# Gamma and beta of layer 0's normalization: two fused VectorE operations in place of two GpSimd operations

## The chip, the cores and the metric

One core of a Trainium2 chip runs the whole program. The metric is device time in microseconds, the median of several executions. The engines of a core have queues of their own that run in order and wait for each other by semaphores: TensorE (PE in the profile; its weight loads are PEld), VectorE (DVE), ScalarE (ACT), GpSimd (POOL) and SyncE (SP), whose queue issues most of the DMAs.

## The reference, cut to what matters

Two cross-attention layers follow each other on 4 x 1024 tokens of width 1024, all in f32. The change concerns the end of layer 0:

```python
# layer 0, after its attention
out = out @ Wo + bo
x = out + hidden_state
mu = jnp.mean(x, axis=-1, keepdims=True)
var = jnp.var(x, axis=-1, keepdims=True)
return (x - mu) * jax.lax.rsqrt(var + EPS) * gamma + beta
# layer 1, with a = norm(audio_kv) * ln_gamma + ln_beta
Q = hidden_states @ Wq.T;  K = a @ Wk.T;  V = a @ Wv.T
out = softmax(Q K^T / 8, masked) V @ Wo.T
return hidden_states + tanh(gate) * out
```

What layer 0 returns is read twice in layer 1: as the left operand of its scores and as the residual.

## The kernel before, in words

The 4096 tokens are 32 subtiles of 128 rows (NSUB); two subtiles are a pair (NPAIR = 16). The program has three parts. First, up to some 720 us, the queries of layer 0 and its attention run, mixed with the folding of layer 1's query weights. Then comes the stage of the change, layer 0's output projection, 16 pairs, with the folding of layer 1's output weights put between (L870, pairs 0 to 7). Last is layer 1, whose scores and outputs alternate by pairs.

A projection of one pair is `project` (L414). The 256 x 1024 by 1024 x 1024 product is made by a Strassen-like scheme: seven products of 128-row, 512-column halves, each four matmuls, into PSUM banks X, V and W that several outputs share. After a product VectorE adds the bank's present content to the rows of one output half (`add`, L430), and the next product accumulates into the same bank. So TensorE's next product into X must wait until VectorE has read X. The order on X is A11*B11, S2*T2, S1*T1, S4*B22; V takes S3*T3 and A22*N4, W takes A12*B21. The left operands S1, S2, S4 and A21-S3 are made by VectorE from the pair's `o` tile in `left_out` (L408 to L411), one pair ahead. In pair 10 and after, VectorE also forms sums of layer 1's weight blocks (L181 to L184, 128x2048 each).

The rows `r` of a pair are loaded from x by SP's queue (L894), and GpSimd adds the output bias bo to them (L895) ahead of the products. When a pair's seven products are added, its normalization runs as filler work between the products of the next pair: `close_rows` (L974) makes a list of steps for each of the two subtiles, and `project` pops a share of them after each product (`others`). The steps are: two bn_stats (L280), then the aggregate, the addition of eps and ScalarE's square root (L285 to L287), then reciprocal and (r - mean) * rstd (L290, L291), then `last`: GpSimd's multiplication by gamma (L977) and addition of beta (L978), and the store of the rows to x1 in DRAM by SP's queue (L979). gamma0_sb and beta0_sb are 128 x 1024 tiles, each row the same.

The r tiles of pairs 1 to 15 come from a pool of six buffers, so the load of a subtile of pair p waits until the x1 store of the same subtile of pair p - 3 has read its buffer. SP's queue issues in the order in which the planner put it; a DMA that waits holds what is behind it. The tile framework that builds the program settles the order of the instructions of each engine from its own estimate of times; bn_stats alone is marked to stay in program order.

Of the kernel before, what the change touches and what calls it, by code (L numbers as in the profile page):

```python
# [11 lines left out]
ALU = mybir.AluOpType  # L12
# [33 lines left out]
EPS0 = 1e-6  # L46
# [25 lines left out]
def tile_two_cross_attentions(  # L72
# [25 lines left out]
    nc = tc.nc  # L98

    def sub_ap(t):  # L100
        return slice(t * P, (t + 1) * P)
# [110 lines left out]
    for i in range(2):  # L212
        t = scratch.tile([P, H], F32, tag="cnat", name=f"ctx_{i}", bufs=2)
# [3 lines left out]
    for w, n in ((wk0, "wk0"), (wv0, "wv0")):  # L217
        t = wpool.tile([P, KC, 256], F32, tag="wb", name=n)
# [3 lines left out]
    def constant(ap, shape, name, dt=F32, pool=const):  # L222
        t = pool.tile(shape, dt, tag=name, name=name)
        nc.sync.dma_start(out=t, in_=ap)
        return t
# [45 lines left out]
    nc.vector.tensor_copy(key_bias, mask1_sb)  # L271
    nc.vector.tensor_scalar(key_bias, key_bias, 1.0, -MASKED, ALU.subtract, ALU.mult)

    def normalize_steps(t, eps, name, late=False):
        st = small.tile([P, 2, 6], F32, tag="st", name=f"st_{name}")
        mv = small.tile([P, 2], F32, tag="mv", name=f"mv_{name}")
        rstd = small.tile([P, 1], F32, tag="rstd", name=f"rstd_{name}")

        def stats(i):
            r = nc.vector.bn_stats(st[:, i, :], t[:, i * 512 : (i + 1) * 512])  # L280
            if late:
                tc.keep_in_program_order(r)

        def deviation():
            nc.vector.bn_aggr(mv, st.rearrange("p a b -> p (a b)"))  # L285
            nc.vector.tensor_scalar(rstd, mv[:, 1:2], eps, None, ALU.add)
            nc.scalar.activation(rstd, rstd, AF.Sqrt)  # L287

        def scale():
            nc.vector.reciprocal(rstd, rstd)  # L290
            nc.vector.tensor_scalar(t, t, mv[:, 0:1], rstd, ALU.subtract, ALU.mult)  # L291

        return [lambda: stats(0), lambda: stats(1), deviation, scale]

    def transpose_ctx(layer):

# [35 lines left out]
    for i in range(2):  # L332
        run(normalize_steps(cnat[i], EPS1, f"ctx{i}", True))
# [475 lines left out]
    steps = query_steps(0, rows)  # L809
# [135 lines left out]
    last = NSUB - SUB  # L945
# [8 lines left out]
    for c in range(2):  # L954
# [12 lines left out]
    gamma0_sb, beta0_sb = (  # L967
        constant(ap.partition_broadcast(P), [P, H], n, F32, c2)
        for ap, n in ((gamma0, "gamma0"), (beta0, "beta0"))
    )  # L970
# [2 lines left out]

    def close_rows(pair, r):  # L974
        def last(u):
            t = pair * 2 + u
            nc.gpsimd.tensor_tensor(r[u], r[u], gamma0_sb, ALU.mult)  # L977
            nc.gpsimd.tensor_tensor(r[u], r[u], beta0_sb, ALU.add)  # L978
            nc.sync.dma_start(out=x1[pair][sub_ap(u), :], in_=r[u])  # L979

        steps = []
        for u in range(2):
            steps += normalize_steps(r[u], EPS0, f"0_{pair * 2 + u}", True) + [lambda u=u: last(u)]
        return steps

    lefts = {}
# [22 lines left out]
    for pair in range(NPAIR):  # L1009
        r, a = ahead_r, ahead_a  # L1010
# [26 lines left out]

        project(a, w_o, r, fill, tail=tail)
        fill = close_rows(pair, r)
        if pair == NPAIR - 2:  # L1040
            xq = load_x1(0)
# [80 lines left out]
    for pair in range(NPAIR):  # L1122
        r = []
# [84 lines left out]
```

## Time and profile before

| what | us |
|---|---|
| median of 3 runs | 1946.02 (1945.31 to 1955.23) |
| the profiled execution, its own time | 1946.74 |
| its span, first to last instruction | 1944.5 |
| TensorE busy, share of the span | 1885.5 (97%) |
| VectorE busy | 1276.9 (66%) |
| ScalarE busy | 384.7 (20%) |
| GpSimd busy | 288.4 (15%) |
| L291, least, median and most of 32 | 0.804, 0.812, 2.956 |
| L977, least, median and most of 32 | 2.342, 2.347, 2.808 |
| L978, least, median and most of 32 | 2.342, 2.357, 4.276 |

The page lists groups of instructions by line, engine and operation, with busy time, mean duration, and the idle time of the engine before them with what ended it. The timeline lists instructions by start; a bracket at the end of a row is the idle time before it and what ended it. The chain that ended last follows the end of the program backwards from each instruction to what released it. The table of stretches gives busy time by engine, TensorE's granted clock as a share of full speed, and the DMA's busy share and rate. One matmul of the source appears as two records in the timeline.

### The profile page before, as it was taken

To read this page: it belongs to the slowest core of one execution; us is meant where nothing else is said; L and a number is where in the kernel's file an instruction comes from. 1 tells how busy PE (TensorE), PEld (TensorE's weight loads), DVE (VectorE), ACT (ScalarE), POOL (GpSimd) and SP (SyncE) were. 2 spreads that over 40 slices of the span, in tenths; PEclk is the share of its full clock that TensorE was granted. 3 is DMA by queue.
4 is the path that set the end of the run, shared out by engine and by line. 5 is a ranking of instruction groups with operands and counts; after the bars stand their busy time and mean duration, and the time that the engine had idled before them with its cause. 6 is when DMAs were issued, how large, how long until landed. Compare 5 with 4: busy or idle time off the path is not lost.

```text
span 1944.5 us, 17115 instructions
## 1 busy us (share of the span) xinstructions
PE 1885.5 (97%) x6160; PEld 892.9 (46%) x6160; DVE 1276.9 (66%) x1540; ACT 384.7 (20%) x1028; POOL 288.4 (15%) x198
## 2 busy tenths in 40 slices
PE   8999999998998889999999999999999999999999
PEld 7744444444445654433443444444444444444444
DVE  3424798898877974454467667557665766576653
ACT  1111554553435761121100001000000000000000
POOL 0000111111100004345445642000000000000000
PEclk9999999999998889999999999999999999999999
DMA  8971689798778885666672335374747474747421
GB/s 278 181 191 65 175 246 262 229 255 243 227 184 247 251 259 187 206 214 201 198 217 98 129 98 140 108 178 124 184 119 184 119 183 125 178 127 176 119 87 43
DMA packets 218180, 342.10 MB, mean 176 GB/s; under 512 B 25456, under 2 KB 140528, under 8 KB 213104
## 3 DMA queue, kind: packets, MB, share of 16 engines
q1 hardware_dynamic: 156736, 255.03, 46.6%
q10 hardware_dynamic: 52544, 46.14, 8.6%
q0 software_dynamic: 8816, 39.85, 7.0%
q8 instruction: 48, 0.79, 0.2%
q14 instruction: 36, 0.29, 0.1%
HBM read 203.34 MB, written 137.63 MB: 175 GB/s over the span
## 4 chain that ended last, share of the span: by engine, by line
PE 81%; DVE 11%; DMA 3%; issue 2%; ACT 2%; SPq 0%; POOL 0%; DVEq 0%; ACTq 0%
PE wx L422 59%; PE wx L558 12%; PE big L662 2%; DVE mx L673 2%; DVE s L666 2%; PE wx L361 1%; PE big L361 1%; PE big L870 1%; DVE s L676 1%; DVE sm L693 1%; DMA q<-qTd 1%; DVE pT L398 1%; DMA pq<-p 1%; DVE s L697 1%; PE wx L843 1%
## 5 line engine op out<-in xcount | busy, mean ns | idle before, releaser
L430 DVE TENSOR_TENSOR r<-wx,r 128x512 f32<-128x512 f32 x224 | 153.8, 687 | 265.5 <-PE wx L422 259.8
L484 ACT ACTIVATE s<-s 128x1024 f32<-128x1024 f32 x32 | 33.7, 1057 | 651.8 <-DVE s L483 642.9
L434 DVE TENSOR_TENSOR s<-wx,key_bias 128x512 f32<-128x512 f32 x64 | 44.2, 690 | 137.2 <-PE wx L422 137.2
L558 PE MATMUL wx<-xT,wq_S 128*128 128x512 f32 x256 | 119.3, 601 | 0.8 <-ACT z L569 0.8
L895 POOL TENSOR_TENSOR r<-r,bo 128x1024 f32<-128x1024 f32 x32 | 78.4, 2458 | 275.1 <-DMA r<-in_x_dram 168.3
L422 PE MATMUL wx<-wo_B,S 128*128 128x512 f32 x256 | 116.7, 599 | 0.9 <-DVE r L430 0.9
L558 PE MATMUL wx<-xB,wq_A 128*128 128x512 f32 x256 | 116.4, 599 | 0.0
L422 PE MATMUL wx<-b_B,pT 128*128 128x512 f32 x256 | 115.8, 593 | 0.6 <-ACT pT L393 0.6
L422 PE MATMUL wx<-b_B,S_p 128*128 128x512 f32 x256 | 116.0, 596 | 0.0
L422 PE MATMUL wx<-a_B,xT 128*128 128x512 f32 x256 | 115.4, 592 | 0.0
L422 PE MATMUL wx<-a_B,S_x 128*128 128x512 f32 x256 | 115.3, 593 | 0.0
L422 PE MATMUL wx<-wo_B,o 128*128 128x512 f32 x256 | 113.5, 595 | 0.0
L680 ACT ACTIVATE s<-s,mx 128x64 f32<-128x64 f32 x304 | 101.1, 335 | 55.2 <-DVE mx L673 49.0
L666 DVE TENSOR_TENSOR s<-big,m 128x1024 f32<-128x1024 f32 x64 | 77.0, 1218 | 41.1 <-PE big L662 41.1
L977 POOL TENSOR_TENSOR r<-r,gamma 128x1024 f32<-128x1024 f32 x32 | 76.5, 2389 | 134.5 <-DVE r L291 134.5
L662 PE MATMUL big<-kv,q 64*128 64x128 f32 x1024 | 86.4, 301 | 10.2 <-DMA q<-qTd 10.0
L662 PEld LDWEIGHTS big<-kv,q 64*128 64x128 f32 x1024 | 75.0, 205 | 44.8 <-issue 36.8
L978 POOL TENSOR_TENSOR r<-r,beta 128x1024 f32<-128x1024 f32 x32 | 80.5, 2514 | 2.4
L398 DVE STREAM_TRANSPOSE pT<-pq 128x1024 f32<-128x1024 f32 x66 | 77.9, 1219 | 1.7 <-DMA pq<-p 1.7
L422 PEld LDWEIGHTS wx<-wo_B,S 128*128 128x128 f32 x256 | 47.3, 190 | 66.6 <-issue 52.9
L697 DVE TENSOR_TENSOR s<-s,sm 128x1024 f32<-128x1024 f32 x64 | 76.8, 1220 | 0.9
L422 PEld LDWEIGHTS wx<-wo_B,o 128*128 128x128 f32 x256 | 48.0, 190 | 63.5 <-issue 63.1
(159 smaller groups left out, 2984.9 us busy)
## 6 DMA issues: line engine op xcount, KB each, us to landing
p<-s POOLq DMA_DIRECT2D x19, 1024.0 KB, 8.6
pq<-p POOLq DMA_DIRECT2D x76, 256.0 KB, 6.0
xq<-in_x_dram SPq DMA_DIRECT2D x64, 256.0 KB, 10.0
q<-qTd SPq DMA_DIRECT2D x32, 512.0 KB, 6.5
oTd<-oT ACTq DMA_DIRECT2D x32, 512.0 KB, 6.7
ad<-a SPq DMA_DIRECT2D x16, 1024.0 KB, 5.8
o<-oTd SPq DMA_DIRECT2D x16, 1024.0 KB, 8.7
r<-in_x_dram SPq DMA_DIRECT2D x32, 512.0 KB, 4.3
```

What stands on the lines that cost most here:

```text
L398: nc.vector.transpose(dst.rearrange("p k (u i) -> p k u i", i=Q), t[:, :, k0 * Q : k1 * Q].rearrange("p u (k j) -> p k u j", j=Q),)
L422: nc.tensor.matmul(bank, a[s][:, k, :], w[m][:, k, :], start=first and k == 0, stop=last and k == HK - 1, skip_group_check=True,)
L430: nc.vector.tensor_tensor(at, bank, at, ALU.add)
L434: nc.vector.tensor_tensor(at, bank.rearrange("p (h s) -> p h s", s=S), bias.unsqueeze(1).to_broadcast([P, 512 // S, S]), ALU.add,)
L558: nc.tensor.matmul(bank, w_q[a][:, k, sub_ap(i)], rows[b][:, k, :], start=first and k == 0, stop=last and k == HK - 1, skip_group_check=True,)
L662: nc.tensor.matmul(ps[:, at : at + P], q[on, c * 4 + g, :], k0bd[on, b, c, :], start=True, stop=True,)
L666: nc.vector.tensor_tensor(quarters[:, :, c * 8 : (c + 1) * 8], ps.rearrange("p (k a l) -> p a k l", a=NQ, l=Q), mask.rearrange("p e (h l) ...
L680: nc.scalar.activation(heads[:, 0, k], heads[:, 0, k], AF.Exp, bias=mx[:, 0, k : k + 1], accum_out=sm[:, 0, k : k + 1],)
L697: nc.vector.tensor_tensor(heads[:, e], heads[:, e], wide(sm[:, e]), ALU.mult)
L895: nc.gpsimd.tensor_tensor(ru, ru, bo_sb, ALU.add)
L977: nc.gpsimd.tensor_tensor(r[u], r[u], gamma0_sb, ALU.mult)
L978: nc.gpsimd.tensor_tensor(r[u], r[u], beta0_sb, ALU.add)
```

## The change: what it does

The multiplication by gamma and the addition of beta leave GpSimd. VectorE computes the same value in two operations with two tensors and one scalar per row: r = (r - mean) * gamma in place of r = (r - mean) * rstd, and then r = r * rstd + beta as a step of its own. The normalization of the context rows keeps the old form. `last` is only the store.

```diff
-    def normalize_steps(t, eps, name, late=False):
+    def normalize_steps(t, eps, name, late=False, scaled=None):
 ...
         def scale():
             nc.vector.reciprocal(rstd, rstd)
-            nc.vector.tensor_scalar(t, t, mv[:, 0:1], rstd, ALU.subtract, ALU.mult)
-
-        return [lambda: stats(0), lambda: stats(1), deviation, scale]
+            if not scaled:
+                nc.vector.tensor_scalar(t, t, mv[:, 0:1], rstd, ALU.subtract, ALU.mult)
+                return
+            nc.vector.scalar_tensor_tensor(t, t, mv[:, 0:1], scaled[0], ALU.subtract, ALU.mult)
+
+        def shift():
+            nc.vector.scalar_tensor_tensor(t, t, rstd, scaled[1], ALU.mult, ALU.add)
+
+        return [lambda: stats(0), lambda: stats(1), deviation, scale] + ([shift] if scaled else [])
 ...
     def close_rows(pair, r):
         def last(u):
-            t = pair * 2 + u
-            nc.gpsimd.tensor_tensor(r[u], r[u], gamma0_sb, ALU.mult)
-            nc.gpsimd.tensor_tensor(r[u], r[u], beta0_sb, ALU.add)
             nc.sync.dma_start(out=x1[pair][sub_ap(u), :], in_=r[u])
 
         steps = []
         for u in range(2):
-            steps += normalize_steps(r[u], EPS0, f"0_{pair * 2 + u}", True) + [lambda u=u: last(u)]
+            steps += normalize_steps(
+                r[u], EPS0, f"0_{pair * 2 + u}", True, (gamma0_sb, beta0_sb)
+            ) + [lambda u=u: last(u)]
         return steps
```

In the changed kernel the two fused operations are lines 295 and 298, and the lines behind them in the file have numbers that are 7 higher in the functions between (L430 is L437 there, L408 to L411 are L415 to L418).

## The prediction

> **What bounds the kernel now.** I read the page first: who is busy, and which rows the change touches. Columns of the rows: busy us, mean ns of one, then the idle time before it.
>
> ```profile
> PE 1885.5 (97%) x6160; PEld 892.9 (46%) x6160; DVE 1276.9 (66%) x1540; ACT 384.7 (20%) x1028; POOL 288.4 (15%) x198
> L895 POOL TENSOR_TENSOR r<-r,bo 128x1024 f32<-128x1024 f32 x32 | 78.4, 2458 | 275.1 <-DMA r<-in_x_dram 168.3
> L977 POOL TENSOR_TENSOR r<-r,gamma 128x1024 f32<-128x1024 f32 x32 | 76.5, 2389 | 134.5 <-DVE r L291 134.5
> L978 POOL TENSOR_TENSOR r<-r,beta 128x1024 f32<-128x1024 f32 x32 | 80.5, 2514 | 2.4
> L697 DVE TENSOR_TENSOR s<-s,sm 128x1024 f32<-128x1024 f32 x64 | 76.8, 1220 | 0.9
> ```
>
> TensorE is the bound, 97% of the span. The change removes the rows L977 and L978, 157 us of GpSimd; L895 stays. None of that is TensorE time, so the question is what TensorE loses in the stage where these rows stand (layer 0's projection, 722 to 1165 us). The table of busy time by stretch, cut at the starts of the pairs, tells it (length, PE, PEld, DVE, ACT, POOL, clock, DMA share, GB/s):
>
> ```profile
> 960.70:1009.70 49.00, 49.00 (x114) 20.98 (x113) 31.91 (x47) 0.81 (x4) 26.50 (x11) 1.00 0.85 236
> 1009.70:1038.70 29.00, 24.65 (x58) 10.26 (x56) 23.86 (x26) 0.41 (x2) 16.50 (x6) 0.98 0.45 173
> 1038.70:1065.90 27.20, 27.20 (x57) 11.74 (x58) 16.18 (x24) 0.41 (x2) 16.69 (x7) 0.89 0.16 58
> 1065.90:1090.30 24.40, 24.40 (x57) 10.42 (x56) 12.04 (x23) 0.41 (x2) 11.49 (x5) 1.00 0.30 108
> ```
>
> A pair without value matmuls takes 24.47 us, two of them 49.0. One takes 29.0, with 4.35 us of idle TensorE, and the next 27.2 at a clock of 0.89. A fourth, from 1090.3, takes 25.4. Pairs 1 to 7, which carry value matmuls (L870), take 29.4 each and wait only for ScalarE. So VectorE costs the stage 4.5 + 2.7 + 0.95 = 8.2 us. The timelines of TensorE, then VectorE, then GpSimd say how:
>
> ```profile
> 1038.69 2.07 PE L422 MATMUL wx<-wo_T,o 128*128 128x512 f32 x2 [4.35 <-DVE o L410]
> 1102.76 2.41 PE L422 MATMUL wx<-wo_B,S 128*128 128x512 f32 x5 [0.87 <-DVE r L430]
> ```
> ```profile
> 1028.12 4.40 DVE L184 TENSOR_TENSOR a_N<-a_B,a_T 128x2048 f32<-128x2048 f32 x1
> ...
> 1033.04 2.24 DVE L408 TENSOR_TENSOR S<-o 128x512 f32<-128x512 f32 x1
> 1035.32 2.71 DVE L409 TENSOR_TENSOR S<-S,o 128x512 f32<-128x512 f32 x1
> 1037.95 0.68 DVE L410 TENSOR_TENSOR o<-o 128x512 f32<-128x512 f32 x1
> ```
> ```profile
> 750.73 9.29 POOL L895 TENSOR_TENSOR r<-r,bo 128x1024 f32<-128x1024 f32 x4 [8.14 <-DMA r<-in_x_dram]
> ...
> 1028.03 2.34 POOL L978 TENSOR_TENSOR r<-r,beta 128x1024 f32<-128x1024 f32 x1
> 1030.33 7.15 POOL L895 TENSOR_TENSOR r<-r,bo 128x1024 f32<-128x1024 f32 x2
> ```
>
> VectorE was stretched: L184 took 4.40 where its kind takes 2.29, L408 and L409 took 2.24 and 2.71 where 0.69 is normal, while GpSimd ran beta and two bo adds beside them. The three stretches add 5.7 us; TensorE waited 4.35 for the L410 behind them. The groups by form show whom GpSimd holds up, the same operation beside it (S) and in layer 1, where GpSimd is idle (S_x):
>
> ```profile
> L411 DVE TENSOR_TENSOR S<-o,S 128x512 f32<-128x512 f32 x16 | 29.0, 1810 | 0.0
> L411 DVE TENSOR_TENSOR S_x<-xT,S_x 128x512 f32<-128x512 f32 x16 | 11.0, 685 | 0.0
> ```
>
> L430, which has one operand in PSUM, stays at 687, and bn_stats (L280) at 681. Stretched are operations with two SBUF tensors, and L291.
>
> **The change, part by part.**
> *Removed on GpSimd:* 64 instructions, 157 us, none on the path. With them go the stretches above, and the wait of the x1 stores (L979, SP queue) for beta. The store of r and the next load of that buffer behind it come earlier, and so does the bo add, which no longer queues behind gamma and beta. Worth up to 8.2 us.
>
> *Added on VectorE:* for each of 32 subtiles one tensor_scalar of 0.81 us becomes two fused operations (L295 and L298 of the changed kernel). The trace has none of that kind. Bounds: 0.81 us below (L291's form; unlikely with a second tensor to read); 2.28 us above. The upper end is a rule against this change: the Trainium skill, "Vector Engine (DVE) Microarchitecture Reference", section 7, says that a scalar-tensor-tensor operation with two non-bf16 sources in SBUF runs at half throughput. Twice 1024 elements at the 0.96 GHz of "VectorE: DVE Perf Modes" plus L697's 0.15 us of fixed cost is 2.28 (an estimate). The nearest row, L697 with two SBUF f32 operands of 1024, shows 1.22, which is one element per cycle. I take 1.22: that row shows both operands arriving at full rate. VectorE gains 32 x (2.44 - 0.81) = 52 us of work; at 16 to 19 of 24.5 us per pair it is still not full.
>
> *Where the new work lies.* In the built order a pair's first half on VectorE is: add to X (L430), two bn_stats, aggregate, L286, L295, reciprocal, L298, then the next add to X, for which TensorE's S1*T1 product waits. Counted from a pair's first S3*T3 matmul (1065.85), the undisturbed pair of before shows where that add must be done:
>
> ```profile
> 1068.89 0.81 DVE L291 TENSOR_SCALAR r<-r,mv,rstd 128x1024 f32<-128x1024 f32 x1
> 1070.64 0.69 DVE L430 TENSOR_TENSOR r<-wx,r 128x512 f32<-128x512 f32 x1 [0.94 <-PE wx L422]
> ```
>
> L286 ends at 2.55; L295 2.6 to 3.8 (it needs no rstd, so ScalarE's root lies under it), reciprocal to 4.0, L298 to 5.2, add to 5.9. S1*T1 starts at 7.1 (1072.96). Slack 1.2 us, so alone the two cost nothing. (gamma and beta are issued at 722.1 and 733.3 and landed by 738, before the first L295 near 757.) Before, the add ended at 5.5. The second half has more: the add before the S4 product now has nothing ahead of it (before, one bn_stats), and the second subtile's L298 ends at 18.4, before the last add at 21.2. In pair 10 the planner puts the two 2.3 us weight sums ahead of that add, but also all of A22*N4 ahead of S4 on TensorE: the add ends near 13 without disturbance, S4 starts at 14.1.
>
> *The bo adds that remain* (32 x 2.35 us) can hold up the fused operations, which have two SBUF tensors. "SBUF — State Buffer", "Who interferes with whom", calls it an exclusive lock for a whole instruction; the trace agrees (2.83 us for the L291 at 757.74). One collision delays by up to 2.35 us; beyond the slack it stalls TensorE by 0.7 to 1.25 us. When does a bo add come? A store lands in 2.9 us, a load in 4.1 (median issue to landing in this stage), so 7.1 us after its L298. For the first subtile that is 12.4: it delays left_out (L408 to L411) and the second L298 to 20.6, harmless. For the second it is 27.7. In a pair of 29.4 us that lies between pairs: free. In one of 24.47 it is 3.3 of the next: GpSimd takes its turn after L295, L298 waits to 6.15 and ends at 7.35, the add at 8.0, a stall of 0.95. One by one: pair 1 (the four bo adds from 750.73 run to about 760) 1.25; pairs 4 and 6 (their load stands behind four bd stores in SP's queue, bo add at about 2.1) 0.7 each; pair 10 (two bo adds push the weight sums) 1.1; pair 11 0.25; pairs 12, 13, 14 0.95 each. Pair 9's load shares the DMA with a_B, 2, 3, 8 and 15 have none at that time. Sum 6.9 us. At the end of the stage four fused operations precede the add that the second score product waits for: 1171.7 against 1171.65, 0.1 us.
>
> *The clock.* "TensorE: Matmul & The Clock Gate", Part 1, halves the clock after an idle window of about 3.4 us. The row agrees for the 4.35 us gap (0.89 in the pair after it); after the gap of 0.87 the 5 us stretches show 1.00. Had each short stall the long one's surcharge (2.7/4.35), 6.9 would be 11; I take 6.9.
>
> *Sum.* The profiled execution took 1946.74 us (span 1944.5 and 2.2 around it), 0.7 over the median of 1946.02. 1946.7 - 8.2 + 6.9 + 0.1 = 1945.5; against the median, 1945.
>
> **The rivals.**
> *The bo adds miss the fused operations* (loads a microsecond later or earlier than I place them; L298 never caught). For: only 71 us of bo adds is left in 443, and a bo add coming before 1.5 or after 5.2 is free. Against: the period is regular, so one hit repeats. 1946 - 8 = 1938 to 1940.
>
> *The late VectorE chain of pair 10 and 11 stays.* For: four weight sums of 2.3 us stand there, and L417 for pair 11 ends at about 24 of 24.5 us; one bo add there makes TensorE idle again, and over 3.4 us the clock falls. Then 4 to 7 of the 8.2 are not saved: 1949 to 1954.
>
> *Slower: the fused operation runs at half rate.* Place: first half of each pair. At 2.28 us L298 ends at 7.35 and S1*T1 waits 0.95 in 14 pairs, 13 us. The slack being gone, the hits count in full, some seven of 2.1, 15 us; the add at the end of the stage comes 4.3 late, with clock 7 us. 1946 - 8 + 35 = 1973. It decides from about 1.8 us per operation, where the slack of 1.2 is used up. For: the sentence quoted. Against: L697.
>
> *A hidden transfer:* x1 is stored earlier, but the chain that ended last has no x1 load in this stage, so nothing is gained: inside the forecast.
>
> **How the numbers follow.** Forecast 0.58; bo adds miss 0.17; late chain 0.12; half rate 0.13. Within 0.5% (9.7 us; about what a measurement can tell from no change) is 1936.3 to 1955.7. Faster needs more than the 8.2 that VectorE costs the stage: 0.03. Slower is half rate and a tail of the late chain: 0.16. Same 0.81. The range runs from the misses, 1937, to the late chain, 1957; half rate is left out. The forecast's own range is 1941 to 1950.
>
> **What would show it.** Right: L295 and L298 at a least time of 1.22, means above 1.3; L411 (L418 there) nearer 0.7 than 1.81; no gap of over 2 us near 1038, clock 1.00; short waits of the S1*T1 weights on VectorE's add in pairs 12 to 14; GpSimd at about 131 us. Wrong: L298 at 2.3, a gap behind L417, or pairs at 24.47 throughout.

## The result, and the profile after

The changed kernel took 1940.2 us, the median of 20 runs (1936.78 to 1945.33), the kernel before beside it 1945.03 us (20 runs, 1940.19 to 1955.23). The ratio is 0.9977, with a 95% interval of 0.9969 to 0.9985: 4.8 us less, which is inside 0.5%. The forecast was 1945, its range 1937 to 1957.

The page of the changed kernel, its busy times and the one group that is left of GpSimd's work in the stage (busy us, mean ns of one, then the idle time before it):

```profile
PE 1880.2 (97%) x6160; PEld 890.1 (46%) x6160; DVE 1307.3 (67%) x1572; ACT 384.6 (20%) x1028; POOL 135.8 (7%) x134
L902 POOL TENSOR_TENSOR r<-r,bo 128x1024 f32<-128x1024 f32 x32 | 82.1, 2571 | 491.9 <-DMA r<-in_x_dram 184.0
```

GpSimd lost 152.6 us, VectorE gained 30.4: less than the 52 of the fused operations, since its other operations are stretched less. The groups by form in the stage (715 to 1170 us) show both:

```profile
L298 DVE SCALAR_TENSOR_TENSOR r<-r,rstd,beta 128x1024 f32<-128x1024 f32 x32 | 48.7, 1523 | 0.6
L295 DVE SCALAR_TENSOR_TENSOR r<-r,mv,gamma 128x1024 f32<-128x1024 f32 x32 | 45.7, 1428 | 0.0
L418 DVE TENSOR_TENSOR S<-o,S 128x512 f32<-128x512 f32 x16 | 10.9, 682 | 0.0
L184 DVE TENSOR_TENSOR a_N<-a_B,a_T 128x2048 f32<-128x2048 f32 x1 | 2.3, 2283 | 0.0
```

L418 is the L411 of before, 1810 ns there. L184 took 4.40 us before. The price of a fused operation is read from one tile's list (least, median and most ns):

```profile
L295 DVE SCALAR_TENSOR_TENSOR r<-r,mv,gamma x32: 1270/1276/3314, 754.9 to 1160.7; 128x1024 f32<-128x1024 f32 x32
```

TensorE's losses: busy time by stretch, cut at the starts of the pairs as before (length, PE, PEld, DVE, ACT, POOL, clock, DMA share, GB/s):

```profile
958.30:1007.25 48.95, 48.95 (x113) 20.96 (x112) 34.17 (x51) 0.81 (x4) 6.08 (x3) 1.00 0.77 214
1007.25:1032.24 24.99, 24.56 (x57) 10.48 (x56) 24.47 (x28) 0.41 (x2) 6.30 (x2) 1.00 0.33 126
1032.24:1057.42 25.18, 24.75 (x58) 10.40 (x56) 18.74 (x25) 0.41 (x2) 8.85 (x3) 1.00 0.39 142
1057.42:1082.60 25.18, 24.75 (x58) 10.40 (x57) 18.73 (x25) 0.41 (x2) 5.13 (x2) 1.00 0.35 125
1082.60:1107.94 25.34, 24.74 (x58) 10.40 (x57) 19.27 (x25) 0.41 (x2) 7.45 (x3) 1.00 0.42 150
1107.94:1132.41 24.47, 24.47 (x57) 10.48 (x56) 17.27 (x27) 0.41 (x2) 0.00 (x0) 1.00 0.14 56
```

Pairs 10 and 11, which took 29.0 and 27.2, take 24.99 and 25.18, and the clock stays at 1.00. Pairs 10 to 13 are over 24.47 by 0.5, 0.7, 0.7 and 0.9, which is 2.8 in all. In place of 8.2, VectorE now costs the stage 2.8. From the start of pair 2 to that of pair 15 the stage went from 356.1 (784.09 to 1140.22) to 350.7 us (781.75 to 1132.41). The profiled executions differ by 7.7 us in span: 5.4 is the stage, and 2.3 was there before pair 1 began (754.69 against 752.36), ahead of anything the change touches. That part is difference between executions: over the thirteen profiles of this case pair 1 begins anywhere from 749.8 to 755.6.

What is left shows in TensorE's timeline as the same wait four times (0.43 in pairs 10 to 12, 0.60 in pair 13). One of them is shown here, with what lies behind it in VectorE's and GpSimd's timelines:

```profile
1039.96 3.70 PE L429 MATMUL wx<-wo_B,S 128*128 128x512 f32 x8 [0.43 <-DVE r L437]
```
```profile
1036.12 3.18 DVE L298 SCALAR_TENSOR_TENSOR r<-r,rstd,beta 128x1024 f32<-128x1024 f32 x1
1039.22 1.28 DVE L437 TENSOR_TENSOR r<-wx,r 128x512 f32<-128x512 f32 x2
```
```profile
1035.37 6.15 POOL L902 TENSOR_TENSOR r<-r,bo 128x1024 f32<-128x1024 f32 x2 [18.84 <-DMA r<-in_x_dram]
```

Pair 11 begins at 1032.24. A bo add starts 3.1 us into it, takes its turn between L295 and L298, and L298 is done 1.9 us late; the add to X behind it makes S1*T1 wait. In pair 14 no bo add comes, L298 takes 1.28, and there is no wait.

### The profile page after: what moved, and what is told of

Its sections match the earlier page's. It is cut to its first block, busy times and chain, and to the rows that moved or that the text cites. A ratio compares the mean times of both kernels' runs of the same rounds, so it can differ in the third digit from the quotient of the medians.

```text
span 1936.8 us, 17075 instructions
## 1 busy us (share of the span) xinstructions
PE 1880.2 (97%) x6160; PEld 890.1 (46%) x6160; DVE 1307.3 (67%) x1572; ACT 384.6 (20%) x1028; POOL 135.8 (7%) x134
## 4 chain that ended last, share of the span: by engine, by line
PE 80%; DVE 12%; DMA 3%; issue 3%; ACT 2%; POOL 0%; SPq 0%; DVEq 0%; ACTq 0%; POOLq 0%
PE wx L429 58%; PE wx L565 12%; PE big L669 2%; DVE mx L680 2%; DVE s L673 2%; PE wx L368 1%; PE big L368 1%; PE big L877 1%; DVE s L683 1%; DVE pT L405 1%; DMA q<-qTd 1%; DVE sm L700 1%; DVE s L704 1%; PE big L740 1%; ACT s L687 1%
## 5 line engine op out<-in xcount | busy, mean ns | idle before, releaser
L437 DVE TENSOR_TENSOR r<-wx,r 128x512 f32<-128x512 f32 x224 | 153.5, 686 | 236.3 <-PE wx L429 223.4
L429 PEld LDWEIGHTS wx<-a_B,S_x 128*128 128x128 f32 x256 | 48.5, 190 | 62.0 <-issue 58.3
L429 PEld LDWEIGHTS wx<-a_B,xT 128*128 128x128 f32 x256 | 48.7, 190 | 61.2 <-issue 60.5
```

Of the source, the lines that this page charges most:

```text
L429: nc.tensor.matmul(bank, a[s][:, k, :], w[m][:, k, :], start=first and k == 0, stop=last and k == HK - 1, skip_group_check=True,)
L437: nc.vector.tensor_tensor(at, bank, at, ALU.add)
```

## The experiments

All were run in five rounds beside the kernel before (1944.2 to 1944.7 us in these batches). One figure compares profiles without the spread ahead of the stage: the time from the start of pair 2 to the start of pair 15, called the stage length here (before 356.1, after 350.7).

### The changed kernel once more

> The changed kernel again, as the base for the others on this chip. Contention theory and every rival: about 1940 us, 0.2% under the kernel before; pairs 10 to 13 take 25.0 to 25.4 us instead of 24.47, because L298 is held up by a bo add (3.2 us instead of 1.28) and the S1*T1 product waits for the add behind it.

1938.71 us, ratio 0.9973 (0.9964 to 0.9982). The stage length is 349.8. The waits of 0.43 came in pairs 10, 11 and 13, none in pair 12, and this time one in pair 1 (0.53, with L295 at 3.27 behind the four bo adds). So which pairs are hit changes from execution to execution; in both profiles it was four.

### The bo adds left out

```diff
-            nc.gpsimd.tensor_tensor(ru, ru, bo_sb, ALU.add)
```

> Leaves out the bo adds on GpSimd, so the output lacks the bias bo; the order of TensorE's and VectorE's instructions is that of the changed kernel. Contention theory: what is left of the loss is the bo adds holding up L298; without them L298 takes 1.28 us everywhere, pairs 10 to 13 return to 24.47 us, and the time falls by 2.8 us against the changed kernel, to about 1937. Rival, the fused operations are simply too long for the first half of a pair: the four waits stay and the time stays at 1940.

1934.66 us, ratio 0.9945 (0.9932 to 0.9959), 4.0 less than the changed kernel beside it, where 2.8 had been expected. Stage length 347.0, 2.8 to 3.7 under the two profiles of the changed kernel. No fused operation is stretched any more:

```profile
L298 DVE SCALAR_TENSOR_TENSOR r<-r,rstd,beta x32: 1274/1283/1286, 755.2 to 1157.3; 128x1024 f32<-128x1024 f32 x32
```

and between pairs 2 and 15 TensorE waits for VectorE nowhere. So what the changed kernel still loses to VectorE comes from the bo adds. The fused operations alone cost nothing, as the forecast had it: 64 of them lie in VectorE's idle time. A pair without value matmuls takes 24.42 here instead of 24.47, though it waits for nothing in either kernel; that is up to 0.9 us over the stage, and its cause stays open.

### The bo adds left out of the kernel before

The same line is removed from the kernel before, where gamma and beta stay on GpSimd.

> The kernel before with the bo adds left out (the output lacks bo); gamma and beta stay on GpSimd. Contention theory: what was added up in pair 10 of the kernel before were two bo adds beside L408 and L409 (3.5 us of stretch) on top of beta beside L184 (2.1 us). Without the bo adds the gap behind L410 shrinks from 4.35 to under 1 us, the clock loss of 2.7 us in the next pair goes, and the time is 1937 to 1941; it stays above the changed kernel without bo adds (1934.7), because gamma and beta still stretch VectorE's operations. Rival, the stage's 8.2 us are due to gamma and beta alone: gap and time stay as before, 1943 to 1945.

1935.69 us, ratio 0.9962 (0.995 to 0.9975), stage length 348.9. That is below the expected 1937 to 1941 and only 1.0 above the changed kernel without bo adds, or 1.9 by the stage lengths (this profile is of the slowest of the five runs, 1939.53). Pair 10 in VectorE's timeline, then TensorE's:

```profile
1028.38 4.41 DVE L184 TENSOR_TENSOR a_N<-a_B,a_T 128x2048 f32<-128x2048 f32 x1
...
1033.31 0.68 DVE L408 TENSOR_TENSOR S<-o 128x512 f32<-128x512 f32 x1
1034.02 0.69 DVE L409 TENSOR_TENSOR S<-S,o 128x512 f32<-128x512 f32 x1
```
```profile
1035.37 1.12 PE L422 MATMUL wx<-wo_T,o 128*128 128x512 f32 x2 [0.77 <-DVE o L410]
```

Beta still stretches L184 to 4.41, and TensorE loses 0.77 to it, with the clock at 1.00. GpSimd's 157 us of gamma and beta therefore cost the stage 1 to 2 us by themselves. The other 7 of the 8.2 need the bo adds: pair 10 is 3.6 shorter without them and pair 11 2.5, which is two bo adds, and pair 13 has lost its wait of 0.87.

The stage lengths of the four kernels do not add up term by term: 356.1 with both kinds of work, 350.7 without gamma and beta, 348.9 without bo adds, 347.0 without either. Leaving out either kind removes most of the loss, since it took both to make it. Why did the two bo adds do less harm when gamma and beta left GpSimd, though they stayed? The next two runs, and the times of the loads, answer that.

### The x1 store held back

```diff
+            nc.gpsimd.tensor_copy(idle[:, 0:1], r[u][:, 0:1])
+            for _ in range(8):
+                nc.gpsimd.memset(idle, 0.0)
+            nc.gpsimd.tensor_tensor(r[u][:, 0:1], r[u][:, 0:1], idle[:, 0:1], ALU.add)
             nc.sync.dma_start(out=x1[pair][sub_ap(u), :], in_=r[u])
```

> The changed kernel, but behind each L298 GpSimd runs a one-column copy, eight writes of a constant into an idle tile (no SBUF source) and a one-column addition into r, and the x1 store waits for that. So the store is held back about as long as gamma and beta held it in the kernel before, while hardly any GpSimd operation reads two SBUF tensors beside VectorE. If two-tensor reads are what costs, and neither GpSimd's writes nor the store's lateness do: 1937 to 1941, like the changed kernel (1938.7), L298 with a least time of 1.27. If the later store, load and bo add cost by themselves: above 1942, with new waits for VectorE's add at the starts of other pairs. If writes block VectorE too: L295 and L298 stretched in most pairs and 1945 or more.

1946.08 us, ratio 1.0013 (1.0005 to 1.0021), stage length 356.7. My theory of that moment, that holding the store back is harmless, fell: the whole gain is gone. The edit changes more than the store, though. The writes stand in GpSimd's queue ahead of the bo adds, and the planner ordered VectorE's work anew: the second L298 of pair 10 stands behind two adds to r, and L184 begins 21.7 us into the pair, where it was 19.6 in the changed kernel. VectorE's timeline in pair 10, GpSimd's, and TensorE's:

```profile
1030.32 2.28 DVE L184 TENSOR_TENSOR a_N<-a_B,a_T 128x2048 f32<-128x2048 f32 x1
...
1033.87 2.82 DVE L417 TENSOR_TENSOR o<-o 128x512 f32<-128x512 f32 x1
1036.62 2.83 DVE L418 TENSOR_TENSOR S<-o,S 128x512 f32<-128x512 f32 x1
```
```profile
1028.54 4.60 POOL L986 MEMSET idle<- 128x512 f32 x8
1033.22 0.19 POOL L987 TENSOR_TENSOR r<-r,idle 128x1 f32<-128x1 f32 x1
1033.36 5.54 POOL L902 TENSOR_TENSOR r<-r,bo 128x1024 f32<-128x1024 f32 x2
```
```profile
1036.75 1.12 PE L429 MATMUL wx<-wo_T,o 128*128 128x512 f32 x2 [3.65 <-DVE o L417]
1040.10 6.17 PE L429 MATMUL wx<-wo_T,S 128*128 128x512 f32 x8 [2.23 <-DVE r L437]
```

L184 is not stretched beside the eight writes of a constant, so these do not hold VectorE up. But GpSimd reaches its two bo adds only at 1033.36, behind the writes, and they meet L417 and L418, which the next pair waits for. It is the picture of the kernel before: there the bo adds came at 1030.33, behind beta. Pair 11 then runs at a clock of 0.88.

### The store held back, without bo adds

The edit before, with the bo add's line removed as well.

> The changed kernel with the x1 store held back as in the run before, but without the bo adds (the output lacks bo). Theory now: what the late store cost there (1946.1 against 1938.7) was only the place that it gave to the two bo adds of pair 10's loads, beside L417 and L418 of that pair. Without bo adds a late store then costs nothing: 1933 to 1937, like the changed kernel without bo adds (1934.7), no gap behind L417, L184 at 2.28 beside GpSimd's writes. If the late store, the loads behind it or GpSimd's writes cost by themselves: 1940 or more, with the gap behind L417 still there.

1935.85 us, ratio 0.9957 (0.9944 to 0.9969), stage length 349.5, L417 at 0.68. In TensorE's timeline a gap is left in pair 10:

```profile
1031.04 1.12 PE L429 MATMUL wx<-wo_T,o 128*128 128x512 f32 x2 [1.49 <-DVE o L417]
```

The order of VectorE's work is that of the run before, so the 10.2 us between these two runs are what the bo adds cost at their late place. The gap of 1.49 comes with the planner's new order: L184 takes 2.28 but begins 21.7 us into the pair, 18.3 in the changed kernel without bo adds. The order, the late store and the writes together cost 1.2 us (1935.85 against 1934.66).

What held the bo adds back, the store or GpSimd's queue? SyncE's timeline and GpSimd's in the kernel before, then GpSimd's in the changed kernel:

```profile
1008.21 1.70 SPq L894 DMA_DIRECT2D r<-in_x_dram  x2
```
```profile
1025.60 2.35 POOL L977 TENSOR_TENSOR r<-r,gamma 128x1024 f32<-128x1024 f32 x1 [7.21 <-DVE r L291]
```
```profile
1010.23 6.30 POOL L902 TENSOR_TENSOR r<-r,bo 128x1024 f32<-128x1024 f32 x2 [20.09 <-DMA r<-in_x_dram]
```

Before, the two loads landed 7.3 and 7.6 us after their issue, by 1017.2. The bo adds began 13 us later, at 1030.33: they stood behind gamma and beta, and gamma behind VectorE's L291. With the store held back the loads had landed by 1018.4 and the bo adds began at 1033.36, behind the writes. So in both it was GpSimd's queue. In the changed kernel, with the store earlier, the loads landed by 4.1 us into pair 10 instead of 7.5. There nothing stands ahead of the bo adds but their loads, and they begin 3.0 us into the pair instead of 20.7. The change gains because GpSimd no longer holds the bo adds back in its own queue.

### Reads on GpSimd that nothing waits for

```diff
             nc.sync.dma_start(out=x1[pair][sub_ap(u), :], in_=r[u])
+            nc.gpsimd.tensor_copy(idle[:, 0:1], r[u][:, 0:1])
+            nc.gpsimd.tensor_tensor(idle, gamma0_sb, beta0_sb, ALU.mult)
+            nc.gpsimd.tensor_tensor(idle, gamma0_sb, beta0_sb, ALU.add)
```

> Adds to the changed kernel, behind each subtile's L298, two GpSimd operations of 128x1024 that read gamma and beta and write a scratch tile nobody reads: GpSimd as busy with reads as before, but no store waits for it; the order on TensorE and VectorE is that of the changed kernel. Contention theory: L182, L184 and L415 to L417 of pair 10 are held up again and TensorE waits near 1032 as it did in the kernel before; 3 to 7 us over the changed kernel, 1943 to 1947. Rival, the gain came from x1 stores and loads that no longer wait for GpSimd: no wait returns, 1940.

1958.69 us, ratio 1.0066 (1.0051 to 1.0081), 20 more than the changed kernel, where 3 to 7 had been expected; stage length 358.4. TensorE's timeline:

```profile
1040.21 2.07 PE L429 MATMUL wx<-wo_T,o 128*128 128x512 f32 x2 [7.25 <-DVE o L417]
...
1177.62 6.38 PE L429 MATMUL wx<-a_B,S_x 128*128 128x512 f32 x8 [4.92 <-DVE s L441]
```

The direction was right and the size was not. I had counted the reads beside the fused operations. The reads also stand in GpSimd's queue ahead of the bo adds of pair 10, which begin only at 1034.08 there. No store waits for GpSimd here and the loads had landed by 1011.5, so the queue alone holds the bo adds back. So L184 (4.38) and L415 (2.23) meet the reads, L416 (2.71) and L417 (2.82) the bo adds, all in one chain, and pair 10 lasts 33.0. A second gap of 4.92 comes where layer 1 begins. Since the bo adds queue behind them, this run does not separate the reads from the bo adds that they delay; the runs without bo adds do.

### The bo add in halves, in the changed kernel and in the kernel before

```diff
-            nc.gpsimd.tensor_tensor(ru, ru, bo_sb, ALU.add)
+            for h in (slice(0, HW), slice(HW, H)):
+                nc.gpsimd.tensor_tensor(ru[:, h], ru[:, h], bo_sb[:, h], ALU.add)
```

In the changed kernel:

> The changed kernel with each bo add made in two halves of 512 columns; the order on TensorE and VectorE is unchanged. Contention theory with turns: VectorE gets in after a half, L298 is delayed by at most 1.2 us instead of 1.9, which the slack of about 1.2 us before S1*T1 takes up; pairs 10 to 13 back to 24.5 to 24.7 us, 2 us under the changed kernel, 1938. Rival, GpSimd keeps its turn for both halves: L298 stays at 3.2 us and the time at 1940.

1934.79 us, ratio 0.9954 (0.994 to 0.9968), 3.9 less than the changed kernel beside it and as low as with no bo adds at all (1934.66). Stage length 348.6. VectorE's timeline in pair 10:

```profile
1012.55 2.33 DVE L298 SCALAR_TENSOR_TENSOR r<-r,rstd,beta 128x1024 f32<-128x1024 f32 x1
```

L298 waits for one half at most: 2.33 at most of 32, where a whole bo add made it 3.18. It is then 1.05 late, which the slack ahead of S1*T1 covers; one wait of 0.50 is left, at a later product of pair 10. The 3.9 us of the medians are more than the stage shows (348.6, against 350.7 and 349.8), in part because the profiled run, 1937.93, is not typical: four of the six took 1934.6 to 1934.9. This version beats both kernels and leaves nothing out.

In the kernel before:

> The kernel before, each bo add in two halves of 512 columns; gamma and beta stay whole on GpSimd. If the two whole bo adds beside L408 and L409 of pair 10 are what the stage of the kernel before loses (8.2 us with the clock), halves let VectorE in sooner: L408 and L409 together at most 3.2 us in place of 4.95, the gap behind L410 at 2.0 to 2.8 in place of 4.35, under the length at which the next pair lost clock, 1938 to 1942. If VectorE has to wait for GpSimd's whole queue: gap and time as before, 1943 to 1946.

1942.24 us, ratio 0.9986 (0.9977 to 0.9994), at the edge of the expectation, and its profile does not support the mechanism: the gap behind L410 was 3.25 instead of 2.0 to 2.8, pair 11 ran at a clock of 0.88, and the stage length is 355.6, only 0.6 better. VectorE's timeline, then GpSimd's:

```profile
1029.40 1.15 DVE L408 TENSOR_TENSOR S<-o 128x512 f32<-128x512 f32 x1
1030.58 1.64 DVE L409 TENSOR_TENSOR S<-S,o 128x512 f32<-128x512 f32 x1
1032.14 1.75 DVE L410 TENSOR_TENSOR o<-o 128x512 f32<-128x512 f32 x1
1033.81 1.75 DVE L411 TENSOR_TENSOR S<-o,S 128x512 f32<-128x512 f32 x1
```
```profile
1026.68 8.33 POOL L896 TENSOR_TENSOR r<-r,bo 128x512 f32<-128x512 f32 x4
```

The two engines take turns, so four short VectorE operations in a row meet the four halves. A half lets one waiting operation in sooner; a chain waits again at each link. The 2.5 us in the medians are more than the stage of this profile shows, and stay unexplained.

### The bo add on VectorE

```diff
-            nc.gpsimd.tensor_tensor(ru, ru, bo_sb, ALU.add)
+            nc.vector.tensor_tensor(ru, ru, bo_sb, ALU.add)
```

> The changed kernel with the bo adds on VectorE too, so that GpSimd does nothing in the stage: 32 times about 1.25 us more VectorE work, 40 us. Contention theory: L295 and L298 at 1.28 throughout, VectorE still has room in each pair, 1934 to 1939, at best as good as the bo adds in halves (1934.8). Rival: VectorE runs in order, so a bo add whose load has not landed holds up what is behind it, and the late chain of pairs 10 and 11 has no room for more: 1943 or more, with gaps behind L417 or VectorE waiting for r's loads.

1940.25 us, ratio 0.9977 (0.9969 to 0.9986): between the two expectations. In the stage it does what contention says, L295 and L298 at most 1.278 and 1.286, stage length 349.0, one loss of 1.89 where two bo adds stand ahead of pair 11's first add. But pair 2 begins at 784.70, 2.95 later than in the changed kernel. The delay is there when the stage begins (the first product at 723.58 against 720.36), where the planner's order differs a little too; whether that order or the execution caused it was not settled. VectorE, running in order, spends 28.2 us waiting for r's loads in front of the bo adds; TensorE's timeline shows no wait that comes of it.

### Each fused operation twice

```diff
-            nc.vector.scalar_tensor_tensor(t, t, mv[:, 0:1], scaled[0], ALU.subtract, ALU.mult)
+            for _ in range(2): nc.vector.scalar_tensor_tensor(t, t, mv[:, 0:1], scaled[0], ALU.subtract, ALU.mult)
```

and the second fused operation in the same way. Without bo adds:

> The changed kernel without the bo adds, each of the two fused operations issued twice in a row (the output is not the normalized row): 2.56 us in place of 1.28, a little over the half rate that the rival named, with no GpSimd beside it. Undisturbed, the add before S1*T1 ended 5.75 into the pair with a start of S1*T1 at 7.1; it now ends at 8.3. Slack theory of the prediction: about 1.2 us of wait in each of 14 pairs, 17 us, and up to 5 at the end of the stage: 1952 to 1960. If the planner's new order or more slack hides it: 1935 to 1940.

1937.56 us, ratio 0.9971 (0.996 to 0.9983), 2.9 above the kernel with single ones, where 17 to 22 had been expected. VectorE's timeline in pair 13 tells why:

```profile
1085.86 0.68 DVE L437 TENSOR_TENSOR r<-wx,r 128x512 f32<-128x512 f32 x1
1086.46 2.60 DVE L298 SCALAR_TENSOR_TENSOR r<-r,rstd,beta 128x1024 f32<-128x1024 f32 x2
```

The planner saw the longer work and put the add to X ahead of both L298. With that order 82 us more of VectorE work lie in idle time, but for one gap of 2.16 behind L417 in pair 10. The half-rate rival meant an operation that is slow on the chip, with the order as it was; here the order changed, so this run is no price of that rival. It shows how much room VectorE has in this stage. With bo adds:

> As before, each fused operation issued twice (the output is not the normalized row), with the bo adds. With the slack gone, a bo add that meets a fused operation counts in full: some seven times 2 us on top of the kernel without the bo adds, so 1966 to 1976 by the working of the rival (1973). If the bo adds still miss most: no more than 4 us above the kernel without them, as with the fused operations issued once.

1946.75 us, ratio 1.001 (1.0003 to 1.0017), 9.2 more than without them, and 8.0 more than the changed kernel. The bo adds cost more the fuller VectorE is, as expected, but not the 1966 to 1976, since the order had changed here too. The profile is of the fastest of the 21 runs, 1941.34, so it shows less than the median lost. In it pair 10 lost most: L298 twice took 6.45 together beside two bo adds, the gap behind L417 was 3.16, and the next pair ran at a clock of 0.94.

## Why the prediction was right, and where it was off

**Right: VectorE's 8.2 us go.** Pair 10 went from 29.0 to 24.99, the gap behind L410 is gone, the clock is at 1.00. The prediction named three ways, the stretch, the store that comes earlier, and the bo add that no longer queues behind gamma and beta, and did not say which carries it. The runs do: it is the queue. Removing the bo adds from the kernel before takes the stage from 356.1 to 348.9 with gamma and beta still there, and making them late again in the changed kernel brings it to 356.7. Of the three stretches that the prediction summed to 5.7 us, the one by beta (L184) alone left a gap of 0.77 of 4.35; the two by bo adds, on top of it, made the rest.

**Right: the fused operations cost nothing alone.** They were put at 1.22 from the row of L697 and measured 1.276 and 1.283, 0.06 us more than that row. The add to X was placed at 5.9 into the pair and ended at 5.75 in pair 14, with S1*T1 at 7.1 as forecast. The slack of 1.2 measures 1.4 to 1.5: L298 was 1.90 late and S1*T1 waited 0.43. The half-rate sentence of "Vector Engine (DVE) Microarchitecture Reference", section 7, would have made it 2.28 by the prediction's estimate; the measurement decides against it for this f32 shape.

**Mis-sized: the bo adds hold up the fused operations, 6.9 us.** The mechanism is right and was seen as described, a bo add about 3 us into the pair that takes its turn after L295. Its size is 2.8 in the profiled execution and 2.7 in the profile of the repeat (pairs 10, 11, 13 and pair 1); the medians with and without bo adds put it at 4.0. By terms:

- Pair 1, 1.25: the four bo adds ran 746.59 to 755.86, and L295 alone was held, for 0.8 us. In the repeat they ran 1.1 later, and the pair lost 0.75.
- Pairs 4 and 6, 0.7 each: nothing. Their bo adds come later than placed: GpSimd's timeline has them at 849.15 and 908.13, 8.5 and 8.6 into their pairs instead of 2.1, and that lies behind L298.
- Pair 10, 1.1: 0.5. Pair 11, 0.25: 0.7, an ordinary hit. Pairs 12 and 13, 0.95 each: 0.7 and 0.9.
- Pair 14, 0.95: nothing. Pair 13's second store was issued at 1096.12, 13.5 into its pair, because the second L298 was ordered before left_out there. Its bo add came at 1102.27, within pair 13. The prediction had put every second L298 at 18.4.

With 2.8 in place of 6.9 the prediction's own sum gives 1946.7 - 8.2 + 2.8 + 0.1 = 1941.4, and 1940.7 against the median; 1940.2 was measured. The forecast's own range began at 1941. A saving of 1 us was forecast and one of 4.8 was measured. The chosen case was therefore right in kind and 4.8 us too high: its net was the small difference of two terms, and the second was about twice too large. The rival in which the bo adds miss (1938 to 1940) lay closer in time, though its mechanism, no hits, is not what the trace shows; the wide range holds the result only because it reaches down to that rival.

**The other rivals.** The late chain of pair 10 and 11 did not stay here, but it was the right place to fear: the store held back, the added reads and the doubled operations each brought that gap back (3.65, 7.25, 3.16). Part of it there is the planner's new order: without bo adds gaps of 1.49 and 2.16 are left in the first and the last. The hidden transfer, x1 stored earlier and nothing gained by it, is not tested alone: no run makes the store early with GpSimd's queue as before. By the landing times the loads of pair 10's bo adds came some 3 us earlier into the pair, and the bo adds themselves 17.7 us.

**What would have shown it.** Least time 1.27 instead of 1.22, means of 1.43 and 1.52 (above 1.3), L418 at 0.68, no gap near 1038, GpSimd at 135.8 instead of 131: as stated. The short waits came in pairs 10 to 13 instead of 12 to 14.

## What to carry to other kernels

Before moving work off an engine because it stretches its neighbours, ask which stretched operation has no slack behind it. Here 157 us of GpSimd work cost 1 to 2 us by themselves, and two bo adds of 2.4 us each cost about 6, since they ran beside the one chain that the next pair waits for, which beta had already made late. What put them there is the queue and the wait ahead of them, so follow a removed operation to what it had been holding back. A short operation on the other engine is cheaper for a single waiting operation, and hardly for a chain.

## What the runs showed of the hardware

- SCALAR_TENSOR_TENSOR with two f32 tensors in SBUF takes 1.28 us for 128x1024, against 1.22 for TENSOR_TENSOR of that shape; no half rate.
- GpSimd writing a constant did not hold up VectorE's addition of two SBUF tensors: L184 took 2.28 us beside writes and 4.40 beside an addition of two tensors.
- With both reading two tensors, the engines alternate instruction by instruction. The wait is the rest of one GpSimd instruction: L298 in pair 10 took 3.18 us beside whole bo adds (2.35 alone) and 2.33 beside halves (1.27 alone).
- The clock in the pair that follows a gap of TensorE in pair 10: 1.00 after 1.49 and 2.16 us, 0.94 after 3.16, 0.89 after 4.35; 0.88 after 3.25 and 3.65, each followed by a second wait (1.15 and 2.23). So in these runs a gap of 2.16 left the clock alone and one of 3.16 did not. A longer gap did not mean a slower next pair: after 7.25 it was 0.94, and the pair with the gap showed 0.94 as well, since part of the slow time passed while TensorE was idle (0.63 from 1035 to 1040, with no matmul in it). In the kernel before that clock was 2.7 of the 8.2 us.
